# Two convolution layers with group norms: the norm of x1 on ScalarE as product and shift instead of on VectorE as subtraction and product

## The chip, the cores and the metric

The kernel runs on one core of a Trainium2 chip. The metric is device time in microseconds (us), the median of several executions. The engines are named as the profile names them: PE (TensorE, matrix products), PEld (its weight loads), DVE (VectorE), ACT (ScalarE), POOL (GpSimd) and SP (SyncE, whose queue issues nearly all the transfers here). "L414" is line 414 of the kernel.

## The reference, cut to what matters

The input x has 8 elements of 8 channels of 512x512 values in fp32. Two layers run one after the other; each adds to x a function of the group-normalized x (4 groups of 2 channels).

```python
def _gn(v, G=4, eps=1e-5):
    B_, C_, H_, W_ = v.shape
    g = v.reshape(B_, G, C_ // G, H_, W_)
    m = jnp.mean(g, axis=(2, 3, 4), keepdims=True)
    s = jnp.var(g, axis=(2, 3, 4), keepdims=True)
    return ((g - m) / jnp.sqrt(s + eps)).reshape(v.shape)

# layer 0: a few low Fourier modes of the normalized x, mixed over the channels
x = x + _L0_conv_ref(_gn(x), L0_conv_T, L0_conv_X, L0_conv_weights1_ri, L0_conv_weights2_ri)
# layer 1: 15 steps of a 3x3 convolution per channel, a hidden convolution, a gate
x = x + _L1_conv_ref(_gn(x), L1_conv_K_local, L1_conv_Wp, L1_conv_bp, ...)
```

Below, x1 is the result of layer 0. Its normalized form, `(x1 - mean) / std` with one mean and one std for each group of two channels, is what layer 1 reads. This normalization is what the change touches.

## The kernel before, in words

A channel of 512x512 values is one tile `xt` of 128 partitions by 2048 values. An element goes through two stages that overlap with those of its neighbours.

Layer 0 of an element (`layer0`, L318) is a Python generator. Each `yield` ends a piece of it, and the pieces are handed out to free PSUM banks in the gaps of the element ahead. For each channel, `over_rows` (L395) makes a small product into PSUM, which ACT copies to SBUF as `ty` (L402). `synthesis` (L425) multiplies `ty` with `e2` on PE (L430), and DVE adds the product to the tile (L433) and takes statistics (L435), in two halves of a tile. After every second channel `close` (L407) is started for the group. In its first piece `group_stats` (L299) averages the means over the partitions with a matmul (L303). In its second piece it does so for the variance (L311), and ACT takes the square root into `std` (L313), with DVE's reciprocal `rstd` after it (L315). Then `close` keeps mean and std for the final output (L410, L411), normalizes the two tiles of the group in place (L414), and puts off the two stores to HBM (`store`, L416 to L421) to the next tick, when they are issued on SP's queue.

Layer 1 reads the stored planes. Its 15 steps run over sets of slabs. A call of `work` (L885) is one tick: two convolutions of a step on PE (`convolve`, L530), the first into the PSUM pairs 0 and 1 and the second into the pairs 2 and 3. Each is followed by `settle`: DVE reads the product (L585) and ACT squares it (L591). In the same tick come one or two rounds of the hidden convolution (L630, evicted by ACT at L636 and DVE at L638), then a piece or two of other work (`others.first`), then the hidden point convolution (L649 into pair 3, read by ACT at L656 or by DVE at L658 with ACT's sigmoid at L662), and one more piece of other work (`others.second`). The pieces of the next element's layer 0 are such other work. ACT also squares whole tiles at the start of a set (L510).

The order matters here. Every engine works through its instructions in the order of the source: `keep_order` (L111) ties each instruction to the one before it on its engine. So if the second piece of `close` is handed out in `others.first`, the next piece there is mostly `over_rows` for the next channel, and then the point convolution and the second half of `synthesis` follow in the same tick. In these lines of `layer0`, `next(closing, None)` is the second piece of `close`, L311 to L414:

```python
                next(closing, None)
                closing = None
            if c + 1 < C:
                yield
                ty_next = over_rows(c + 1)
            yield LONG
            synthesis(ty, xt, st[:, c % 2], 1)
```

After the last group of an element no `over_rows` follows. With 8 elements of 4 groups, `close` runs 32 times and L414 runs 64 times. The first element has its layer 0 in a prologue of its own, with no other work beside it; the other seven lie beside the steps of the element ahead.

Of the kernel before, what the change touches and what calls it, by code (L numbers as in the profile page):

```python
# [35 lines left out]
F32 = mybir.dt.float32  # L36
AF = mybir.ActivationFunctionType
ALU = mybir.AluOpType
# [3 lines left out]
P = 128  # L42
# [84 lines left out]
def conv_layers(ctx: ExitStack, tc: tile.TileContext, a, out):  # L127
    nc = tc.nc
# [5 lines left out]
    sm = ctx.enter_context(tc.tile_pool(name="small", bufs=1))  # L134
# [33 lines left out]
    def later(ticks, work):  # L168
        put_off.append((now[0] + ticks, work))
# [84 lines left out]
    shift = prep[:, 0:96].rearrange("p (d o) -> p d o", d=3)  # L254
# [44 lines left out]
    def group_stats(mv, n, bank):  # L299

        mean = sm.tile([P, n], F32, name=f"mean{n}")
        ps = bank[-1][:, 0]
        nc.tensor.matmul(ps[:, :n], avg, mv[:, :, 0], start=True, stop=True)  # L303
        nc.vector.tensor_copy(mean, ps[:, :n])
        var = sm.tile([P, n], F32, name=f"var{n}")
        nc.vector.tensor_tensor(var, mv[:, :, 0], mean, ALU.subtract)
        nc.vector.tensor_tensor(var, var, var, ALU.mult)
        nc.vector.tensor_tensor(var, var, mv[:, :, 1], ALU.add)
        yield LATER
        ps = bank[-1][:, 0]  # L310
        nc.tensor.matmul(ps[:, :n], avg, var, start=True, stop=True)  # L311
        std = sm.tile([P, n], F32, name=f"std{n}")
        nc.scalar.activation(std, ps[:, :n], AF.Sqrt, bias=eps)  # L313
        rstd = sm.tile([P, n], F32, name=f"rstd{n}")
        nc.vector.reciprocal(rstd, std)  # L315
        return mean, rstd, std

    def layer0(e, bank):  # L318
# [9 lines left out]
        for c in range(C):  # L328
            yield c
            xt = e.x[c]  # L330
# [13 lines left out]
        mean, rstd, _ = yield from group_stats(mv, G, bank)  # L344
# [62 lines left out]
        def close(g, mv):  # L407

            mean, rstd, std = yield from group_stats(mv, 1, bank)
            nc.vector.tensor_copy(means[:, 0, g : g + 1], mean)  # L410
            nc.vector.tensor_copy(means[:, 1, g : g + 1], std)  # L411
            for c in (2 * g, 2 * g + 1):
                xt = e.x[C + c]
                nc.vector.tensor_scalar(xt, xt, mean, rstd, ALU.subtract, ALU.mult)  # L414

                def store(c=c, xt=xt):  # L416
                    nc.sync.dma_start(
                        out=e.xn[1 : N + 1, c].rearrange("(p j) w -> p j w", j=4), in_=xt
                    )
                    e.done_with(C + c)  # L420
                    e.stored += 1  # L421

                later(1, store)
# [15 lines left out]
        for c in range(C):  # L439
            yield C + c  # L440
            ty, xt = ty_next, e.x[C + c]
            if c % 2 == 0:
                st = sm.tile([P, 2, 4, 6], F32, name="st1", bufs=2)
            synthesis(ty, xt, st[:, c % 2], 0)
            if closing:
                yield LATER
                next(closing)
                yield LATER
# [7 lines that stand above are left out]
            if c % 2:  # L456
                closing = close(c // 2, aggregate(st, 1))
# [549 lines left out]
```

## Time and profile before

| what | value |
|---|---|
| median of 3 runs (lowest to highest) | 10038.94 us (10036.4 to 10042.99) |
| profiled execution, own time | 10041.66 us |
| its span, first to last instruction | 10039.9 us |
| mean granted clock of PE | 0.982 |
| L591, squares of the steps on ACT | 2240 instructions, mean 1055 ns |
| L585, DVE's read of the steps' product | 2400 instructions, mean 1219 and 1220 ns |
| L402, copy of ty on ACT | 64 instructions, mean 579 ns |
| L313, square root on ACT (128x1) | 32 instructions, mean 261 ns |
| table loads on ACT ahead of L313 / ahead of L662 | 36 / 36, 1283 ns each |

How to read it: "busy" of an engine is the time in which it had an instruction running. A group of instructions is listed with its total busy time, the mean of one, and the idle time of the engine just before, with what ended it. The chain of waits follows the work back from the last instruction, at each step to what released it; its shares say which engine set the end. In a timeline, neighbouring instructions of one line are merged and counted (x2).

### The profile page before, as it was taken

What the parts mean: (1) busy time and instruction counts of PE and PEld (TensorE: products, weight loads), DVE (VectorE), ACT (ScalarE), POOL (GpSimd) and SP (SyncE); (2) the same over time, 40 slices, a digit from 0 to 9 for tenths busy, and PEclk for the clock granted to TensorE, in tenths of its full rate; (3) what the DMA queues carried; (4) which work ended last, traced back from release to release, by engine and by line L of the source; (5) the groups of instructions that cost most, each with busy time, mean ns of one, the idle gap of its engine ahead of it and who ended that gap; (6) DMA issues with size and microseconds to landing.
All of it is one profiled execution on the core that took longest, in us unless ns stands there. A gap on an engine that the chain in (4) does not pass through costs nothing.

```text
span 10039.9 us, 353554 instructions
## 1 busy us (share of the span) xinstructions
PE 9402.8 (94%) x160496; PEld 4310.8 (43%) x160496; DVE 5831.1 (58%) x6067; ACT 4299.0 (43%) x4445; POOL 1761.6 (18%) x1406
## 2 busy tenths in 40 slices
PE   6998999999999999999999999999999999998999
PEld 3444444444444444444444444444444444444433
DVE  5655555755557555665556655566555665555555
ACT  2444444444444444444444444444444444444422
POOL 2010111202111031111212012120121201212212
PEclk9999999999999999999999999999999999999999
DMA  5231255546555465544655455553556635654588
GB/s 170 81 83 50 61 140 150 153 105 148 136 151 150 111 154 133 154 139 115 149 140 154 123 130 142 141 163 119 132 140 146 170 101 136 155 138 102 134 196 200
DMA packets 625565, 1353.51 MB, mean 135 GB/s; under 512 B 73066, under 2 KB 73194, under 8 KB 594050
## 3 DMA queue, kind: packets, MB, share of 16 engines
q1 hardware_dynamic: 621728, 1329.77, 51.5%
q8 instruction: 1261, 20.66, 0.9%
q14 instruction: 238, 1.95, 0.1%
q10 hardware_dynamic: 2338, 1.13, 0.0%
HBM read 992.27 MB, written 268.78 MB: 126 GB/s over the span
## 4 chain that ended last, share of the span: by engine, by line
PE 81%; DMA 7%; DVE 5%; issue 4%; ACT 2%; POOL 1%; SPq 1%; ACTq 0%; POOLq 0%; DVEq 0%
PE pair L530 38%; PE pair L630 24%; PE pair L700 8%; PE pair L649 7%; PE pair L717 3%; DVE h L638 2%; DMA cml<-m 2%; DMA dO<-xn 1%; ACT h L636 1%; DMA dE<-xn 1%; PE pair L430 1%; DVE x L433 1%; DVE mix L710 0%; DVE st L435 0%; DVE m L585 0%
## 5 line engine op out<-in xcount | busy, mean ns | idle before, releaser
L530 PE MATMUL pair<-m,band 32*32 32x512 f32 x115200 | 4122.6, 611 | 157.5 <-issue 77.7
L591 ACT ACTIVATE m<-m 128x1024 f32<-128x1024 f32 x2240 | 2359.2, 1055 | 2751.3 <-DVE m L585 2605.1
L530 PEld LDWEIGHTS pair<-m,band 32*32 32x32 f32 x115200 | 2281.5, 104 | 1918.1 <-issue 1043.4
L630 PE MATMUL pair<-cols,w_p 32*128 32x511 f32 (+1 forms) x24576 | 2846.1, 601 | 29.2 <-DMA cols<-xn 14.5
L585 DVE SCALAR_TENSOR_TENSOR m<-pair,dO 128x1024 f32<-128x1024 f32 x1280 | 1507.4, 1219 | 1370.1 <-PE pair L530 1167.2
L585 DVE SCALAR_TENSOR_TENSOR m<-pair,dE 128x1024 f32<-128x1024 f32 x1120 | 1319.4, 1220 | 1195.8 <-PE pair L530 1050.0
L630 PEld LDWEIGHTS pair<-cols,w_p 32*128 32x128 f32 x24576 | 1275.0, 186 | 1612.4 <-issue 1086.0
L638 DVE TENSOR_SCALAR h<-pair,b_p 128x1024 f32<-128x1024 f32 x1024 | 1313.4, 1283 | 786.7 <-PE pair L630 778.5
L636 ACT ACTIVATE h<-pair,b_p 128x1024 f32<-128x1024 f32 x1024 | 1140.5, 1114 | 907.6 <-PE pair L630 906.2
L649 PE MATMUL pair<-h,w_u 128*32 128x512 f32 x8192 | 1008.5, 603 | 211.7 <-DVE h L638 186.4
L723 POOL TENSOR_TENSOR mix<-mix 96x512 f32<-96x512 f32 x344 | 437.5, 1272 | 4049.0 <-ACT mix L721 3659.9
L700 PE MATMUL pair<-gin,w_g 128*32 128x511 f32 (+1 forms) x8256 | 964.3, 600 | 16.0 <-DMA gin<-nca 8.0
L705 POOL TENSOR_TENSOR mix<-mix 96x512 f32<-96x512 f32 x344 | 441.5, 1283 | 1879.4 <-DMA mix<-nca 1596.1
L595 POOL TENSOR_SCALAR dO<-dO 128x2048 f32<-128x2048 f32 x80 | 434.0, 5439 | 1148.0 <-DVE m L585 1140.7
L649 PEld LDWEIGHTS pair<-h,w_u 128*32 128x32 f32 x8192 | 252.1, 110 | 852.5 <-issue 363.0
L662 ACT ACTIVATE y<-y,b_u 128x512 f32<-128x512 f32 x256 | 184.8, 722 | 899.4 <-DVE y L658 899.4
L700 PEld LDWEIGHTS pair<-gin,w_g 128*32 128x32 f32 x8256 | 235.1, 110 | 694.3 <-issue 468.4
L656 ACT COPY y<-pair 128x512 f32<-128x512 f32 x256 | 149.8, 585 | 633.0 <-PE pair L649 507.5
L710 DVE TENSOR_SCALAR mix<-pair,b_g 128x512 f32<-128x512 f32 x344 | 258.1, 750 | 260.3 <-PE pair L700 260.3
L717 PE MATMUL pair<-mix,w_g 128*32 128x512 f32 x2064 | 358.2, 595 | 50.8 <-DVE mix L710 49.1
L728 DVE SCALAR_TENSOR_TENSOR mix<-mix,back 96x512 f32<-96x512 f32 x344 | 310.0, 901 | 141.6 <-POOL mix L723 141.6
L658 DVE TENSOR_TENSOR y<-y,pair 128x512 f32<-128x512 f32 x256 | 175.0, 683 | 280.5 <-PE pair L649 268.8
(85 smaller groups left out, 2676.5 us busy)
## 6 DMA issues: line engine op xcount, KB each, us to landing
gin<-xn SPq DMA_DIRECT2D x344, 384.0 KB
cols<-xn SPq DMA_DIRECT2D x256, 512.0 KB
x<-in_x SPq DMA_DIRECT2D x120, 1024.0 KB
gin<-cml SPq DMA_DIRECT2D x344, 320.0 KB
gin<-nca SPq DMA_DIRECT2D x344, 320.0 KB
dE<-xn SPq DMA_DIRECT2D x320, 256.0 KB
dO<-xn SPq DMA_DIRECT2D x320, 256.0 KB
mix<-xn SPq DMA_DIRECT2D x344, 192.0 KB
```

The lines of the kernel that those rows point to most:

```text
L530: nc.tensor.matmul(ps[h // 2][32 * t : 32 * t + 32, h % 2], band[at, c0 + (t if step % 2 else h), dx], m[at, t, dx : dx + N], start=(n == ...
L585: nc.vector.scalar_tensor_tensor(u[:, at], ps[q], FLOOR, d[:, at], ALU.max, ALU.add)
L591: nc.scalar.square(u[:, at], u[:, at])
L595: nc.gpsimd.tensor_scalar(d, d, 0.5, None, ALU.add)
L630: nc.tensor.matmul(ps[g // 2][:, g % 2, lo:hi], w_p[p, dx, i % 2], self.cols[p, i // 2, at : at + hi - lo], start=(n == 0), stop=(n == 2), ...
L636: nc.scalar.activation(h[:, :2], ps[0], AF.Relu, bias=b_p)
L638: nc.vector.tensor_scalar(h[:, 2:], ps[1], b_p, 0.0, ALU.add, ALU.max)
L649: nc.tensor.matmul(ps[32 * g : 32 * g + 32], w_u[:, r % 4], h[:, g], start=(r == self.hs[0][0]), stop=(r == self.hs[-1][0]), tile_position ...
L700: nc.tensor.matmul(ps[32 * j : 32 * j + 32, lo:hi], gband[:, dx], gin[:, j, at : at + hi - lo], start=(n == 0), stop=(n == 2), tile_positi ...
L705: nc.gpsimd.tensor_tensor(d, d, ng, ALU.subtract)
L717: nc.tensor.matmul(ps[at], gpoint[:, at], mix[:, 3], start=True, stop=True, tile_position=(0, 32 * j),)
L723: nc.gpsimd.tensor_tensor(d, d, mix[: GR * C, 2], ALU.mult)
```

## The change

After the reciprocal, DVE makes a per-partition `shift = (mean * -1) * rstd`. The two tiles of the group are then normalized by ACT as `Identity(x * rstd + shift)`, in place as before, at the same position in the source. Everything else stays: the two copies for the output, the stores, their delay of one tick, the number of tiles.

```diff
         def close(g, mv):
 
             mean, rstd, std = yield from group_stats(mv, 1, bank)
+            shift = sm.tile([P, 1], F32, name="shift")
+            nc.vector.scalar_tensor_tensor(shift, mean, -1.0, rstd, ALU.mult, ALU.mult)
             nc.vector.tensor_copy(means[:, 0, g : g + 1], mean)
             nc.vector.tensor_copy(means[:, 1, g : g + 1], std)
             for c in (2 * g, 2 * g + 1):
                 xt = e.x[C + c]
-                nc.vector.tensor_scalar(xt, xt, mean, rstd, ALU.subtract, ALU.mult)
+                nc.scalar.activation(xt, xt, AF.Identity, bias=shift, scale=rstd)
 
                 def store(c=c, xt=xt):
                     nc.sync.dma_start(
```

## The prediction

> **What bounds the kernel now.** I read the page first (engine shares, the chain that ended last), then the groups by line and shape, then who waits for line 402, then the timeline around all 32 normalizations, and last the granted clock by window.
>
> ```profile
> PE 9402.8 (94%) x160496; PEld 4310.8 (43%) x160496; DVE 5831.1 (58%) x6067; ACT 4299.0 (43%) x4445; POOL 1761.6 (18%) x1406
> ...
> PE 81%; DMA 7%; DVE 5%; issue 4%; ACT 2%; POOL 1%; SPq 1%; ACTq 0%; POOLq 0%; DVEq 0%
> ```
>
> TensorE is the bound: 94% busy and 81% of the chain. DVE (58%) and ACT (43%) have room on average, so what counts is whether TensorE waits for them at the 32 places that the change touches.
>
> ```profile
> L510 ACT ACTIVATE m<-dE,mhalf 128x2048 f32<-128x2048 f32 x80 | 159.6, 2000 | 174.3 <-POOL m L509 129.6 <-DMA cml<-m 44.4
> L414 DVE TENSOR_SCALAR x<-x,mean,rstd 128x2048 f32<-128x2048 f32 x64 | 83.7, 1350 | 0.0
> L313 ACT ACT_TABLE_LOAD x36 | 46.2, 1283 | 0.6
> ```
>
> L414 is what leaves DVE: 64 instructions, 1350 ns each, 83.7 us. L510 is the nearest row to what ACT gets: one ACTIVATE of 128x2048 f32, 2000 ns.
>
> Now the place itself, the third channel group of one element. The columns are start, duration, engine, line, operands, and in brackets the idle time before and its releaser.
>
> ```profile
> 4457.38 0.26 ACT L313 ACTIVATE std<-pair,eps 128x1 f32<-128x1 f32 x1
> 4457.54 0.58 ACT L402 COPY ty<-pair 128x512 f32<-128x512 f32 x1
> 4457.67 0.16 DVE L315 RECIPROCAL rstd<-std 128x1 f32<-128x1 f32 x1 [1.44 <-ACT std L313]
> ...
> 4457.87 2.60 DVE L414 TENSOR_SCALAR x<-x,mean,rstd 128x2048 f32<-128x2048 f32 x2
> ...
> 4458.15 1.25 PE L430 MATMUL pair<-e,ty 8*128 8x512 f32 x4
> 4458.33 0.59 ACT L656 COPY y<-pair 128x512 f32<-128x512 f32 x1 [0.21 <-ACT ty L402]
> ...
> 4459.33 6.58 PE L530 MATMUL pair<-m,band 32*32 32x512 f32 x192
> 4460.39 1.21 DVE L433 TENSOR_TENSOR x<-x,pair 128x1024 f32<-128x1024 f32 x1
> ...
> 4462.84 2.34 DVE L585 SCALAR_TENSOR_TENSOR m<-pair,dO 128x1024 f32<-128x1024 f32 x2
> ```
>
> On ACT the copy of ty (L402) stands directly behind the square root (L313); TensorE's L430 reads ty, and all later matmuls stand behind L430. Today ty is ready 0.48 us after the root's end at 4457.64 (called t0 below), and L430 starts at t0+0.51, as soon as L649 is through. So the slack in front of L430 is nearly nothing. The view of line 402 says the same: waits that ended on ty are counted on TensorE.
>
> ```profile
>   PEld pair L430: 23.2, 16
>   PE pair L430: 11.6, 8
> ```
>
> Last, the clock (PEclk is the share of full speed granted):
>
> ```profile
> core 0: us, PE busy (x) PEld busy (x) DVE busy (x) ACT busy (x) POOL busy (x), PEclk, DMA share, GB/s
> 4457.64:4466.00 8.36, 8.36 (x208) 4.37 (x204) 7.56 (x11) 2.91 (x4) 0.00 (x0) 1.00 0.68 250
> 4408.44:4419.30 10.86, 10.81 (x200) 5.29 (x200) 7.58 (x10) 2.23 (x3) 0.00 (x0) 0.69 0.75 264
> ```
>
> ```profile
> 4410.13 9.19 PE L530 MATMUL pair<-m,band 32*32 32x512 f32 x192
> ```
>
> At 4408, where TensorE had already waited for the root and ty, the 192 matmuls of L530 took 9.19 us instead of 6.58, at clock 0.69: a stall of TensorE is paid for a second time.
>
> **What the Trainium skill says.** "TensorE: Matmul & The Clock Gate", section on the HAM clock gate: after an idle window of about 3.4 us the array runs at half clock until it has been busy for about as long. The trace agrees, and is harsher: the page before shows half clock after waits of only 1.5 to 2.4 us, as at 4408. "ScalarE: Activation LUTs", section "Table sets": copy, relu and identity are in every table set. The trace agrees for what it has: copy (L402, L656), square (L591) and relu (L636) run after a root without a load; Identity itself is in no row. The same page, section "What ACT_TABLE_LOAD costs": each per-partition pointer operand adds about 93 ns, and neighbours overlap by as much. The trace has the one-pointer form (L510, 2.00 us); two of L510 in a row start 1.9 us apart.
>
> **The change part by part.** *Small vector work:* one shift of 128x1 follows the reciprocal: 0.16 us like L307, 0.19 with the gap between dependent ones. It starts at t0+0.23 and ends at t0+0.40. Against it, DVE loses 2.60 us at each place. *The new wait:* the first ACT norm waits for shift and starts near t0+0.45. *The norms:* a pointer scale is not in the trace; from below 2.00 us (L510, scale an immediate), from above 2.09 (plus 93 ns); I take 2.08, and 1.99 from start to start. The pair ends at t0+0.45+1.99+2.08 = 4.52. Everything behind it on ACT waits: L402 now ends at t0+5.01 instead of 0.48 (+4.53), L656 behind it as well. Queued behind L402 on TensorE: L430 and the step's L530; behind these DVE's L585 and the squares L591.
>
> The 32 places, from the timelines:
>
> (a) 13 places in the middle of the run where a point convolution L649 precedes L430 and the clock is full (six at group 0, seven like the one shown). L430 starts at t0+5.04. L530 then starts at t0+6.22; it starts today at t0+1.93 on average in the first six (+4.29) and at 1.65 in the seven (+4.57). Sum 6x4.29 + 7x4.57 = 57.7 us. TensorE idles about 4.2 to 4.5 us, more than a whole clock window, so the half clock follows. By the phase of the free-running windows, 3.0 to 6.4 us of later work run at half speed, on average about 4.6, costing half: 2.3 us (2.6 were paid at 4408). 13x2.3 = 29.9 us.
>
> (b) 8 places where TensorE waits and goes cold already (seven without L649 in front, one at 460 us). L430 moves by 4.53, less 0.1 because the cold time after an already cold start is not longer: 7x4.4 = 31. At 460 us L430 is held by L649 until t0+1.25 today: +3.75. Sum 34.6 us.
>
> (c) 7 last groups: no L402 follows, but L656 does, and it frees the pair that the second convolution of the step writes. Today that convolution starts at t0+0.51+3.29 = 3.80; L656 will end at t0+5.02. Stall 1.2 us, too short for the clock in most: 8.4 us.
>
> (d) 4 in the prologue, where nothing else runs. Three times L402 waits only for L398 and ends at t0+2.2; now t0+5.01: +2.8 each. DVE's adds (L433) follow it and set the pace there, so its lost 2.60 us buy nothing: the norm ran while DVE waited for L430 anyway (0.8 us of idle remain). The last one moves the store of xn, for which the first cols load waits, from t0+3.2 to 4.52: +1.3. Sum 9.7 us.
>
> DVE's relief in (a): L585 is held today by L414, L433 and L435 in front of it until t0+5.20, but the first convolution ends at t0+1.69+3.29 = 4.98. At most 0.2 us could be gained, and it lies inside the longer stall. The stores on SP (L417) come up to 1.3 us later, and what is queued behind them (cols, m<-m, x loads) has several us and moves with TensorE. The sigmoid's table load and the squares behind the norms end before the late L585.
>
> Sum: 57.7 + 29.9 + 34.6 + 8.4 + 9.7 = 140 us. The profiled execution took 10041.66 us (span 10039.9), 2.7 above the median of the runs shown, 10038.94; on that median: 10179, and I say 10180.
>
> **The rivals.** *The clock stays up* in most places of (a): then 30 us less, 10150. For it: some windows with 45 to 55% of TensorE busy stayed at full clock. Against it: an idle stretch of 4.2 us is longer than any window. *Delay partly absorbed:* a third of the 110 us of pure delay is made good where TensorE later waits for a load or DVE at a time the stall doesn't move: 10140. Against it: nearly all those waits end on work which TensorE itself feeds. *Identity needs its own table:* one more load of 1.28 us per place, plus a reload for the sigmoid in some: 32x1.28 = 41 more, 10220. *Not slower:* the unloaded DVE decides. It needs L402 and L656 to reach ACT before the norms, or ty to be unneeded for 4.5 us; then only the relief counts: 0.2 us at 13 places, 2.6 at 4 in the prologue, 13 us, 10026. It takes over where L430's slack is above 4.5 us; the trace shows 0.0 to 0.7 us.
>
> **How the numbers follow.** Forecast as summed 0.62; clock stays up 0.15; partly absorbed 0.13; own table 0.06; not slower 0.04. The bounds: norms 2.00 to 2.09 us (3 us in all), the clock's cost 0 to 3.2 us per place of (a) (−30 to +12), the absorbed third −37, more table work +41. The range of 8 in 10 is 10120 to 10222. A measurement of this kernel can tell about 0.2%, 20 us, from no change. Slower by more than that 0.95, within 0.03, faster 0.02.
>
> **What would show it.** Right: an ACT group of 64 Identity instructions near 2.0 us each with no table loads beyond 36; TensorE waiting some 4 us for ty at 20 places; L530 at about 9 us behind those of (a); L585 waiting for TensorE there; a mean clock below 0.982. Wrong: L430 starting within 1 us of the root, L402 ahead of the norms on ACT, or L530 still 6.6 us after the stall.

## The result, and the profile after

The changed kernel takes 10142.88 us (median of 4 runs, 10124.14 to 10152.67) against 10040.97 us before: a ratio of 1.0102, 95% interval 1.0085 to 1.0120. It is slower by 102 us. The profiled execution took 10141.48 us (its span is 10139.5 us), 99.8 us more than the 10041.66 us of the profiled execution before.

From the page of the changed kernel, the busy time by engine and the shares of the chain that ended last:

```profile
PE 9421.1 (93%) x160496; PEld 4300.0 (42%) x160496; DVE 5758.3 (57%) x6035; ACT 4432.6 (44%) x4509; POOL 1759.2 (17%) x1406
...
PE 78%; DMA 8%; DVE 5%; issue 4%; ACT 3%; SPq 1%; POOL 1%; ACTq 0%; POOLq 0%; DVEq 0%
```

DVE has 73 us less to do and ACT 134 us more. TensorE's busy time hardly rose (18 us), so most of the 100 us is time in which TensorE stands. The groups of the changed kernel say what ACT got (the lines below the change have moved down by two, L430 is now L432 and L530 is L532):

```profile
L416 ACT ACTIVATE x<-x,shift,rstd 128x2048 f32<-128x2048 f32 x64 | 130.6, 2088 | 13.7 <-DVE shift L411 13.7
L313 ACT ACT_TABLE_LOAD x36 | 46.2, 1283 | 0.6
L411 DVE SCALAR_TENSOR_TENSOR shift<-mean,rstd 128x1 f32<-128x1 f32 x32 | 5.2, 161 | 1.1
```

Each norm takes 2088 ns, shift 161 ns, ACT waits 0.43 us for shift each time, and there is no further table load. Who waits for the copy of ty on ACT (us in all, times):

```profile
  PEld pair L532: 80.8, 27
  PE pair L532: 55.4, 21
  PEld pair L432: 29.9, 15
  PE pair L432: 16.1, 11
```

Before, TensorE's eight waits on this copy were L430's, one at the first channel of each element and none at the 32 places; the weight loads of L530 had 0.6 us. Now the matmuls of the step's convolution wait for it 21 times, at the 13 places of (a) and the 8 of (b). L432 has its eight old waits and three new ones in the prologue. The timeline of the changed kernel at the place that the prediction shows (third group of the same element; the root ends at 4508.25, which is t0):

```profile
4507.99 0.26 ACT L313 ACTIVATE std<-pair,eps 128x1 f32<-128x1 f32 x1
...
4508.68 4.08 ACT L416 ACTIVATE x<-x,shift,rstd 128x2048 f32<-128x2048 f32 x2 [0.42 <-DVE shift L411]
4508.76 1.25 PE L432 MATMUL pair<-e,ty 8*128 8x512 f32 x4
4509.94 1.05 PE L532 MATMUL pair<-m,band 32*32 32x512 f32 x4
...
4512.67 0.56 ACT L402 COPY ty<-pair 128x512 f32<-128x512 f32 x1
4513.13 0.58 ACT L658 COPY y<-pair 128x512 f32<-128x512 f32 x1
...
4513.28 8.86 PE L532 MATMUL pair<-m,band 32*32 32x512 f32 x188 [2.29 <-ACT ty L402]
4518.97 2.36 DVE L587 SCALAR_TENSOR_TENSOR m<-pair,dO 128x1024 f32<-128x1024 f32 x2 [6.37 <-PE pair L532]
```

L432 runs at t0+0.51 as before, four microseconds ahead of L402: it doesn't need this ty. TensorE then issues four records of the convolution (two matmuls, each of two records) and stands until L402 has ended. In the code, `over_rows` in the middle of a tick makes `ty_next`, while the second half of `synthesis` still works with the `ty` of the current channel. What L402 holds up is the PSUM pair that it reads: the convolution's first two matmuls write pair 0, its third is the first to write pair 1, and the small product lies there until L402 has read it. So it is at all 13 places of (a).

At the eight places of (b) the tick has only one hidden round, and there `work` hands pair 0 to `over_rows`. So the convolution's first matmul already has to wait, again behind an L432 that has long started (the root ends at 4455.11 here):

```profile
4455.16 2.10 PE L432 MATMUL pair<-e,ty 8*128 8x512 f32 x4 [1.39 <-ACT std L313]
4460.14 2.76 PE L532 MATMUL pair<-m,band 32*32 32x512 f32 x33 [2.88 <-ACT ty L402]
```

The windows view of the stretch from 4508.25, at the third group, gives the granted clock (PEclk, 1.00 at this place before):

```profile
core 0: us, PE busy (x) PEld busy (x) DVE busy (x) ACT busy (x) POOL busy (x), PEclk, DMA share, GB/s
4508.25:4522.20 13.95, 11.65 (x208) 5.28 (x204) 5.37 (x10) 6.94 (x7) 0.00 (x0) 0.76 0.41 152
```

At a last group, where no L402 follows, the read of the point convolution holds the second convolution at its third matmul, after 100 records:

```profile
4551.25 3.88 PE L532 MATMUL pair<-m,band 32*32 32x512 f32 x100
...
4555.16 0.56 ACT L658 COPY y<-pair 128x512 f32<-128x512 f32 x1
...
4555.78 3.37 PE L532 MATMUL pair<-m,band 32*32 32x512 f32 x92 [0.64 <-ACT y L658]
```

Since all the kernels here give TensorE the same matmuls in the same order, the start of the nth matmul can be compared between two traces. The growth of that lag within 14 us of L311 at each place gives the loss by the prediction's classes:

| class | predicted, us | measured, us |
|---|---|---|
| (a) 13 places with full clock | 87.6 (57.7 stall, 29.9 clock) | 58.7 (40.4 stall, 18.3 clock, less what was made good) |
| (b) 8 places already cold | 34.6 | 22.5 |
| (c) 7 last groups | 8.4 | 9.2 (1.3 each) |
| (d) prologue | 9.7 | 5.9 |
| everywhere else | 0 | 3.5 |
| sum | 140 | 99.8 |

The stall in (a) is worked out from the timelines: the third matmul starts at t0+5.03 everywhere, and would have started 0.14 us after the convolution, whose start before was t0+1.78 on average, so 13 x 3.11 = 40.4. Of each 3.1 us TensorE is idle for 2.0 to 2.7 us by the record.

### The profile page after: what moved, and what is told of

Its sections match the earlier page's. It is cut to its first block, busy times and chain, and to the rows that moved or that the text cites. A ratio compares the mean times of both kernels' runs of the same rounds, so it can differ in the third digit from the quotient of the medians.

```text
span 10139.5 us, 353565 instructions
## 1 busy us (share of the span) xinstructions
PE 9421.1 (93%) x160496; PEld 4300.0 (42%) x160496; DVE 5758.3 (57%) x6035; ACT 4432.6 (44%) x4509; POOL 1759.2 (17%) x1406
## 4 chain that ended last, share of the span: by engine, by line
PE 78%; DMA 8%; DVE 5%; issue 4%; ACT 3%; SPq 1%; POOL 1%; ACTq 0%; POOLq 0%; DVEq 0%
PE pair L532 36%; PE pair L632 24%; PE pair L702 7%; PE pair L651 7%; PE pair L719 2%; DMA cml<-m 2%; DVE h L640 1%; DMA dO<-xn 1%; ACT h L638 1%; DMA dE<-xn 1%; DMA mix<-nca 1%; ACT x L416 1%; DVE m L587 1%; DMA mix<-xn 1%; DVE x L435 0%
## 5 line engine op out<-in xcount | busy, mean ns | idle before, releaser
L532 PE MATMUL pair<-m,band 32*32 32x512 f32 x115200 | 4142.1, 612 | 230.0 <-issue 84.4
L532 PEld LDWEIGHTS pair<-m,band 32*32 32x32 f32 x115200 | 2277.6, 104 | 2023.9 <-issue 1070.5
L638 ACT ACTIVATE h<-pair,b_p 128x1024 f32<-128x1024 f32 x1024 | 1141.3, 1115 | 882.6 <-PE pair L632 863.3
L597 POOL TENSOR_SCALAR dO<-dO 128x2048 f32<-128x2048 f32 x80 | 434.5, 5445 | 1159.4 <-DVE m L587 1159.3
L658 ACT COPY y<-pair 128x512 f32<-128x512 f32 x256 | 149.9, 585 | 632.5 <-PE pair L651 491.3
```

Of the source, the lines that this page charges most:

```text
L532: nc.tensor.matmul(ps[h // 2][32 * t : 32 * t + 32, h % 2], band[at, c0 + (t if step % 2 else h), dx], m[at, t, dx : dx + N], start=(n == ...
L597: nc.gpsimd.tensor_scalar(d, d, 0.5, None, ALU.add)
L638: nc.scalar.activation(h[:, :2], ps[0], AF.Relu, bias=b_p)
```

## The experiments

Three theories were set against each other. A: ACT works in order, so L402 and L656 end late and the PSUM pairs that they read are not free for the step's convolutions. B: the work that ACT gets costs time wherever it stands. C: the hand-over costs, that is the wait for shift and the later stores. The table gives all kernels: the measured ratio to the kernel before, and from the profiled execution the lag of TensorE in us, in all, at the prediction's classes, in the later part of the six ticks at group 0 of elements 3 to 8 (14 to 26 us after the matmul L311, against the mean of the three profiles of before), and beside all these.

| kernel | ratio (95% interval) | all | (d) | (a) | (b) | (c) | group 0, later | rest |
|---|---|---|---|---|---|---|---|---|
| changed kernel | 1.0102 (1.0085 to 1.0120) | 99.7 | 5.9 | 58.7 | 22.5 | 9.2 | 0.1 | 3.3 |
| norms at the end of the tick | 1.0022 (1.0014 to 1.0030) | 20.5 | 6.0 | -4.1 | -0.6 | 0.0 | 10.9 | 8.3 |
| the same once more | 1.0025 (1.0016 to 1.0035) | 14.9 | 6.4 | -4.8 | -2.6 | 0.0 | 12.3 | 3.6 |
| one norm on ACT, one on DVE | 1.0042 (1.0026 to 1.0058) | 43.6 | 0.7 | 25.8 | 6.5 | 0.0 | 0.0 | 10.6 |
| copy of ty on DVE | 1.0020 (1.0013 to 1.0027) | 19.2 | 1.0 | -1.4 | -2.2 | 9.2 | 6.3 | 6.3 |
| 20 idle copies | 1.0152 (1.0137 to 1.0166) | 145.1 | 8.9 | 91.6 | 39.6 | 22.9 | 0.0 | -17.9 |
| 14 idle copies | 1.0098 (1.0082 to 1.0114) | 91.1 | 4.2 | 64.3 | 20.7 | 9.1 | 0.0 | -7.2 |
| end of tick, first element on DVE | 1.0018 (1.0008 to 1.0027) | 27.4 | -1.1 | -5.1 | -4.9 | 0.0 | 12.3 | 26.2 |
| norms on DVE, end of tick | 1.0013 (1.0005 to 1.0021) | -15.1 | -0.2 | 10.3 | -6.0 | 0.0 | 0.4 | -19.6 |
| 14 idle copies, end of tick | 1.0041 (1.0029 to 1.0054) | 18.9 | 4.1 | -0.8 | 0.6 | 0.0 | 37.6 | -22.6 |
| the same once more | 1.0031 (1.0019 to 1.0043) | 12.9 | 4.2 | -0.6 | -0.9 | 0.0 | 33.9 | -23.7 |
| before, second profile | none (one run) | 7.8 | -0.4 | 1.0 | -2.3 | 0.0 | 0.0 | 9.5 |
| before, third profile | 0.9999 (0.9990 to 1.0008) | -0.1 | 0.0 | 0.6 | -3.1 | 0.0 | 0.2 | 2.2 |

The three profiles of one program differ by some 10 us in the last column and by up to 3 us in (a) and (b), so these columns are read only where they are larger.

**The norms at the end of the tick.** The same instructions on ACT, put behind L402 and L656:

```diff
-                nc.scalar.activation(xt, xt, AF.Identity, bias=shift, scale=rstd)
+                def norm(xt=xt):
+                    nc.scalar.activation(xt, xt, AF.Identity, bias=shift, scale=rstd)
+
+                later(1, norm)
```

> The two norms stay on ACT and still wait for shift, but are issued at the end of the tick, behind the copy of ty (L402) and the read of the point convolution (L656). Theory A (ACT works in order, so L402 and L656 end late and the PSUM pairs they read are not free for the step's convolutions): the main part is as before, only the prologue's 7 us stay, 10048 us, 10035 to 10060. Theory B (the 134 us of work that ACT gets cost time wherever they stand): about 10140. Theory C (the hand-over counts: the wait for shift, the later store of xn, which comes another 2 us later here): about 10140.

It took 10062.09 us against 10039.61, 2 us above A's range and far from B's and C's 10140. Classes (a), (b) and (c) lose nothing any more, with ACT's work, the shift and late stores all still there. B and C fall as the cause of the 100 us. The 22 us that stay are more than the prologue's 6; they are taken up below.

**One norm on ACT, one on DVE**, at the place of the change:

```diff
-                nc.scalar.activation(xt, xt, AF.Identity, bias=shift, scale=rstd)
+                if c % 2:
+                    nc.scalar.activation(xt, xt, AF.Identity, bias=shift, scale=rstd)
+                else:
+                    nc.vector.tensor_scalar(xt, xt, mean, rstd, ALU.subtract, ALU.mult)
```

> The first tile of a group is normalized by DVE as before, the second by ACT, at the place of the change. Theory A: L402 ends about 3.0 us after the root, 1.25 us after the third matmul of the convolution wants its pair: 13 times 1.25, 8 times 1.1, nothing at the last groups since L656 ends ahead of the second convolution, 2 in the prologue, hardly any half clock: 27 us in all, 10068 (10055 to 10080). Theory B: half of the loss, 10090. Theory C: the whole loss, 10140, since shift is waited for as before.

It took 10082.51 us, 43 more than before: 2.5 us above A's range, and nearer to B's 50 than to A's 27. The time alone does not decide between the two. By place it is A: nothing at the last groups, where half of the changed kernel's loss would have been 4.6, and 1.0 to 1.4 us at seven of the 13 places of (a). The other six lost 2.1 to 3.6. Their timeline shows a second gap in the middle of the convolutions (this is the third group of the third element):

```profile
2011.54 1.05 PE L535 MATMUL pair<-m,band 32*32 32x512 f32 x4
...
2012.90 5.37 PE L535 MATMUL pair<-m,band 32*32 32x512 f32 x143 [0.31 <-ACT ty L402]
...
2019.40 2.18 PE L535 MATMUL pair<-m,band 32*32 32x512 f32 x45 [1.13 <-issue]
```

The first gap is L402's, as expected. The second is put down to "issue", that is to nothing that the profile shows, and A had not foreseen it. The traces do show where such gaps lie. If every instruction of TensorE's queue is counted (weight loads, matmuls and waits), all 59 gaps over 0.5 us of this kind, except the first, lie a multiple of 256 instructions apart, to within one. So do those of the kernel before, 51 with 84.5 us in all, of which none falls within 14 us of a place; here they are 100.5 us, and six fall there. They belong to fixed points of the instruction stream. Why such a point costs time in one run and not in another is not shown.

**The copy of ty on DVE**, all else as in the changed kernel:

```diff
-            nc.scalar.copy(ty.rearrange("k p j -> k (p j)"), ps)
+            nc.vector.tensor_copy(ty.rearrange("k p j -> k (p j)"), ps)
```

> As the changed kernel, with the copy of ty (L402) made by DVE, so that the norms on ACT stand in front of L656 alone. Theory A: pair 1 is free 1.2 us after the root, before the convolution wants it; L656 ends at 4.97 us, just when the second convolution wants pair 3, and is late only at the 7 last groups (9 us); 10052 us, 10040 to 10065. Theory B: ACT still has the norms, 37 us of copies less: 10110 to 10140. Theory C: 10140.

It took 10059.93 us, inside A's range. The same place in its timeline (t0 is 4459.10):

```profile
4459.53 4.08 ACT L416 ACTIVATE x<-x,shift,rstd 128x2048 f32<-128x2048 f32 x2 [0.43 <-DVE shift L411]
4459.53 0.68 DVE L402 COPY ty<-pair 128x512 f32<-128x512 f32 x1
4459.60 1.25 PE L432 MATMUL pair<-e,ty 8*128 8x512 f32 x4
4460.78 6.71 PE L532 MATMUL pair<-m,band 32*32 32x512 f32 x192
...
4463.51 0.56 ACT L658 COPY y<-pair 128x512 f32<-128x512 f32 x1
```

The norms stand on ACT just as in the changed kernel, but pair 1 comes free at t0+1.1, and the 192 records run through in 6.71 us. Pair 3, which L658 frees, is just in time here and still 1.3 us late at the seven last groups, the 9.2 us of class (c). So the late end of L402 is the whole of (a) and (b): with this one instruction on another engine both are gone. That TensorE waits for the pair and not for the data of ty is read from the code and from the timelines, where L432 runs ahead of L402.

**Idle copies.** The kernel before, with the norms on DVE and no shift, and small copies to a tile that nobody reads in ACT's queue behind the root:

```diff
+            for _ in range(20):
+                nc.scalar.copy(spare, band.rearrange("p c d o -> p (c d o)")[:, :P])
             nc.vector.tensor_copy(means[:, 0, g : g + 1], mean)
```

> The kernel before (norms on DVE, no shift) with 20 copies of 128x128 to a tile that nobody reads put on ACT behind the root, about 4.1 us each time. Theory A: L402 ends some 4.5 us after the root, 0.4 us earlier than in the changed kernel, with the same stalls otherwise: 85 us, 10125 (10105 to 10140). Theory B: about 10140. Theory C: 10041, since nothing is handed over and no store moves.

It took 10189.54 us, 150 more than before, out of A's range and far from C's. The size of the block was wrong: a copy took 297 ns, and neighbours did not overlap (0.33 us from start to start). So it was made again with 14 copies:

> The run with the idle copies on ACT took 0.297 us a copy, 5.95 us for 20, not the 4.1 intended. Here 14 copies, 4.17 us, so that L402 ends about 4.65 us after the root, where the changed kernel has 4.97. Theory A (the pairs come free late because ACT works in order): the stalls of the changed kernel less 0.3 us each: a 13 times about 4.2, b 8 times about 2.5, c 7 times 1.0, prologue 6: 88 us, 10128 (10115 to 10140). Theory C (wait for shift, later stores): 10040. If the 20 copies cost 150 us by something other than the length of ACT's block, this one should not come down by 60.

It took 10130.27 us, a ratio of 1.0098. In its timeline the block of copies ends at t0+4.48, where the pair of norms ends at t0+4.51 in the changed kernel (t0 is 4509.08, L403 is the copy of ty):

```profile
4508.98 4.58 ACT L412 COPY spare<-band 128x128 f32<-128x128 f32 x14
...
4510.77 1.05 PE L533 MATMUL pair<-m,band 32*32 32x512 f32 x4
...
4513.46 0.58 ACT L403 COPY ty<-pair 128x512 f32<-128x512 f32 x1
...
4514.10 2.77 PE L533 MATMUL pair<-m,band 32*32 32x512 f32 x33 [2.28 <-ACT ty L403]
```

The copy of ty ends at t0+4.96 here and at t0+4.97 in the changed kernel, and the loss is about the same by place and in all. Work that computes nothing, waits for nothing and moves no store costs as much as the norms: what counts is how long ACT is taken in front of L402 and L656. DVE still makes its norms here, and the loss is not larger than in the changed kernel, so the time that the change frees on DVE bought nothing that shows.

**What the late norms still cost.** The first element's norms on DVE again, all others on ACT at the end of the tick:

```diff
-                later(1, norm)
+                if e.b:
+                    later(1, norm)
+                else:
+                    nc.vector.tensor_scalar(xt, xt, mean, rstd, ALU.subtract, ALU.mult)
```

> The norms on ACT at the end of the tick, and in the prologue on DVE as before. Theory A: the prologue's 6 us go away against the same run with ACT in the prologue: 10056 if the 16 us that it had beside the prologue belong to late norms and stores, 10041 if they were scatter between executions. No more than 0.1% below the kernel before in either case, since DVE was not the bound.

It took 10055.43 us against 10037.4: by place the prologue's part is gone, and some 18 us are still there. A second profile of the kernel before should say what is scatter:

> The kernel before once more, for a second profile: how far TensorE's place in time scatters between two executions of one program, away from the 32 places. Expected 10020 to 10062, with steps of up to 7 us in either direction along the run and none at the 32 places.

It took 10049.42 us, with steps of up to 6 us along the run and none over 1.6 us at the 32 places. Then two kernels that part late stores from late work on ACT, the kernel before with its DVE norms issued through `later(1, norm)`, and the kernel before with the 14 idle copies issued through `later(1, idle)`:

> The norms on DVE as before, but issued at the end of the tick, with their stores. Open is where some 16 us come from that the kernel with late norms on ACT has beside the prologue. If late norms and stores cost them: 10055 here too. If ACT's 134 us of work cost them wherever they stand: 10040 here. Theory A for the 32 places: none of them moves.

> The kernel before with the 14 idle copies on ACT (4.17 us each time) at the end of the tick, behind L402 and L656. Theory A: the 90 us that the same copies cost behind the root are gone but for the prologue's 4: 10042. If ACT's work costs some us wherever it stands: 10055.

The first took 10038.95 us against 10027.55 on its chip, the second 10062.08. Late DVE norms cost 10 us at (a), where none had been expected, and nothing in the later part of the ticks. L585, which reads the next product, now stands behind them; at group 0 of the third and fourth elements the hidden round (L630) waits 1.43 us for it. The idle copies cost nothing at the 28 places outside the prologue and yet 0.4% in all, where A had expected 10042. The last two questions were put once more on one chip, with the kernel before as its own comparison:

> The kernel before, as its own comparison on the chip of the next two runs. A ratio of 1.000 within its interval; what it differs from 1.000 is what the comparison itself can be wrong by.

> The 14 idle copies at the end of the tick once more. If ACT's late work costs time that no place shows: 1.003 to 1.004 again, and against the profile of before from the same chip a lag that grows away from the 32 places. If the first figure came from the chip or the day: 1.000 to 1.001, the prologue's 4 us.

> The late norms on ACT once more, on the same chip: 1.002 again if the unplaced 16 us are the kernel's, 1.0006 (the prologue's 6 us) if they were scatter.

They gave 0.9999, 1.0031 and 1.0025. So the cost is the kernels' own, and the traces have its main place: the group-0 ticks, 14 to 26 us after L311. There ACT squares two whole tiles (L510, some 4 us for both) behind the norms. The timeline of the late norms, in their second profile, at group 0 of the fifth element (L516 is L510 of before, L597 is L591, L642 is L636, L644 is L638, L436 is L430):

```profile
4357.43 4.07 ACT L418 ACTIVATE x<-x,shift,rstd 128x2048 f32<-128x2048 f32 x2
...
4361.40 3.88 ACT L516 ACTIVATE m<-dE,mhalf 128x2048 f32<-128x2048 f32 x2
...
4365.18 2.93 ACT L597 ACTIVATE m<-m 128x1024 f32<-128x1024 f32 x3
...
4366.43 1.28 DVE L644 TENSOR_SCALAR h<-pair,b_p 128x1024 f32<-128x1024 f32 x1 [0.46 <-PE pair L636]
...
4368.02 1.09 ACT L642 ACTIVATE h<-pair,b_p 128x1024 f32<-128x1024 f32 x1
...
4369.16 1.25 PE L436 MATMUL pair<-e,ty 8*128 8x512 f32 x4 [0.26 <-ACT h L642]
```

ACT has no gap from the norms to L642, the eviction of a hidden round, and L436 wants the pair that L642 reads. DVE starts its half of this eviction (L644) as soon as the matmuls are done, ACT 1.6 us later. In the kernel before, ACT had been idle for 0.37 us when the same matmuls ended, and started together with DVE:

```profile
4372.53 1.11 ACT L636 ACTIVATE h<-pair,b_p 128x1024 f32<-128x1024 f32 x1 [0.37 <-PE pair L630]
```

The stall of TensorE over L436 and L398 is 0.7 us in all, and the clock falls to half behind it, from 4372.2 on for 6.8 us. The three profiles of the kernel before have full clock at this place. The windows of the late norms' trace show 0.53 from 4372 to 4376:

```profile
4372.00:4376.00 4.00, 4.00 (x16) 0.75 (x8) 1.08 (x2) 0.64 (x2) 0.00 (x0) 0.53 0.35 135
```

So at the place shown this, too, is theory A, one tick part later and at another pair. The group-0 ticks make 11 to 12 us of the 15 to 27 us that the three traces with late norms lag, and the prologue makes 6 where its norms are on ACT. The idle copies lose 34 to 38 us there, three times as much, and why was not followed; elsewhere their traces take back some 23 us. About half of that is gaps put down to "issue", which sum to 73.2 and 71.6 us in these two traces against 84.5 to 86.9 in the three of the kernel before. No kernel with norms on ACT came below the kernel before.

## Why the prediction was right, and where it was off

- *TensorE is the bound, and the place counts, not the averages.* Right. ACT stayed at 44% busy.
- *Price of the norms, shift and wait.* Right: 2088 ns for 2080, the first norm at t0+0.43 for 0.45, L402's end at t0+4.97 for 5.01, no table load. The second pointer operand added 88 ns to L510's 2000, close to the 93 ns that the Trainium skill gives in "ScalarE: Activation LUTs", section "What ACT_TABLE_LOAD costs".
- *"TensorE's L430 reads ty, and all later matmuls stand behind L430."* This is the step that failed. L430 works with the ty of the channel before and starts, at the place shown, at t0+0.51 as it did before. The wait is that of the convolution for the PSUM pair, of its third matmul in (a) and of its first in (b), and TensorE waits 2.6 us on average at the 21 places, not some 4. One of the prediction's own signs of being wrong, L430 starting within 1 us of the root, came true. The 1.25 us of L430 were therefore counted a second time behind the stall: 4.3 to 4.6 us per place in (a), where it is 3.1, and 4.4 in (b), where it is 2.8. That is 29 of the 40 us by which the forecast was too high. The direction survived since both readings have L402 behind the norms on ACT. That the time still fell inside the range is luck as far as this step goes: the range was made wide for other reasons, the clock and an absorbed third. The view of line 402 was read too quickly: its eight waits of L430 on ty are all at the first channel of an element, and the line of L430 in the timeline shown has no wait on it.
- *The half clock after the stall.* Right in kind, too large in size. The stall is 3.1 us and not 4.5. The half clock lasted 3.4 us at ten places, 6.8 at two, and did not come at one: 48 us at half speed, which cost about 24 us where 29.9 were predicted in (a). At four places TensorE made good 1.1 to 1.5 us of its lag within the 14 us, 5 us in all, which leaves the 18.3 of the table. The Trainium skill, in the section of "TensorE: Matmul & The Clock Gate" on the HAM clock gate, speaks of a whole idle window of about 3.4 us; here 2.0 to 2.7 us of idle time were followed by half clock at 12 of 13 places, and so was, in the late norms at 4369, a stall of 0.7 us among small matmuls (L430 with 8 rows, L398 with 16).
- *(c), the second convolution behind L656.* Right: 1.2 us predicted, 1.3 measured at each of the seven.
- *(d), the prologue.* 2.6, 2.6 and 2.5 us between the roots for the 2.8 predicted; the last step did not get longer: the first matmul on cols comes 13.27 us after the last root, and came 14.12 us after it before, so the 1.3 us predicted there are not seen. Why was not tried.
- *DVE's relief buys nothing.* Right as far as the idle copies can tell, which cost no more than the change although DVE keeps its norms.
- *The rivals.* The clock staying up is excluded at 12 of the 13 places, the extra table load for all. "Partly absorbed" would have met the number (10140), but only in small part by its mechanism: some 5 us were made good in (a), not a third of 110, and the stall was smaller from the start.

## What to carry to other kernels

Before work is moved to an engine with free time, look at what stands behind it in that engine's queue, and whether one of those instructions frees a PSUM buffer that TensorE is about to write. Then follow which version of a double-named buffer (ty and ty_next) a consumer really reads: a consumer in the same tick may need the old one, and the wait can then be for the buffer's space and not, as was forecast here, for its data. If such work must go to the busy queue, put it behind the evictions, and look for the next ones that it then delays.

## What the runs showed of the hardware

- A pair of ACTIVATEs with per-partition scale and bias on 128x2048 f32 took 4.08 us; 2088 ns for one. Twenty copies of 128x128 f32 to one tile took 297 ns each and did not overlap (0.33 us from start to start).
- At one place the half clock came after a stall of TensorE of only 0.7 us among matmuls of 8 and 16 rows (0.53 in 4372 to 4376). Behind the stalls of 3.1 us in (a) it lasted 3.4 us at ten of 13 places.
- In all 14 traces TensorE has gaps with no releaser in the profile: 43 to 59 that are longer than 0.5 us, 72 to 100 us in a run. But for at most two in each trace they lie at a multiple of 256 instructions from each other in TensorE's queue. What makes them, and why most such points cost nothing, is not shown.
